# Two-layer graph attention: scores and aggregates by one level of Strassen, VectorE's side work in small pieces

## Chip, cores, metric

One core of one Trainium2 chip. The metric is the device time of one execution, in microseconds (us); each kernel ran several times on one chip with the kernel before.

## The reference, cut to what matters

N = 2708 nodes, D = 1024 features, all float32; adj is an N x N 0/1 matrix.

```python
h = relu(layernorm(x))
e = relu((h @ Wf + bf) @ (h @ Wg + bg).T)          # scores, N x N
att = softmax(where(adj > 0, e, NEG), axis=1)
x = x + att @ (h @ W0 + bW)                         # layer 0
h = relu(layernorm(x))
g = h @ W1
e = leaky_relu(g @ a1 + (g @ a2).T)                 # layer 1: scores are a sum of two vectors
x = x + relu(softmax(where(adj > 0, e, NEG), axis=1) @ g)
```

Both kernels work out `q = h Wf Wg^T` once, scores as `q h^T`, and take the product with W0 or W1 after the aggregate (`(att h) W`). So three large products run over N x N x D: the scores, and one aggregate in each layer.

## The kernel before

Nodes are cut into six panels of columns (four of 512, two of 330) and 22 tiles of up to 128. A panel's scores need 22 x 8 matmuls, and so does each aggregate.

```python
# rows: 6 buffers of 4 KB a partition, slots: 74 of 2 KB
for p in range(NP):                       # preamble, panel by panel
    ...                                   # load x, normalise, transpose: hp
    ...                                   # project: q_ps -> q_ev -> q_d in DRAM
    ...                                   # load adj, convert (nm), transpose: mask in DRAM

def scores(p):
    for t in range(NT):
        nc.sync.dma_start(hT[:, :, :n], hT_d[t][:, :, :n])
        ps = bank("s_ps")
        for k in range(NC):
            nc.tensor.matmul(ps[:n, :w], hT[:, k, :n], q[k][:, :w], ...)
        nc.vector.tensor_tensor(s, ps, nrb, OP.max)      # then + mask, then running max
    ...

def aggregate(l, p, Pt, then={}):
    for c in range(NC):
        ps = bank("g_ps")
        for t in range(NT):               # cut: loads of hc
            nc.tensor.matmul(ps[:, :w], hc[:n, t - t0, :], Pt[t][:n, :w], ...)
        copy(g[:, :w], ps[:, :w])
    ...

def finish0(r):                           # after the projection of each tile of layer 0
    ...                                   # residual, store, normalise for layer 1,
    ...                                   # dots with a1 and a2, running max over the masks

for p in range(NP):
    scores(p + 1); aggregate(0, p, ...); project(p, ..., finish0)
```

## Time and profile before

| | before |
|---|---|
| time, median | 3790.3 us |
| PE busy / DVE busy | 94% / 34% |
| scores of one panel, 512 / 330 columns | 151.1 / 97.9 us, PE never idle |
| first scores begin / second panel's scores begin | 582 / 789 us |
| from an aggregate's last matmul to the projection's first | 4.9 to 5.3 us, ten times (weights); none at two narrow panels |

The profile's lines for this stand in the prediction. PE is TensorE, DVE VectorE, ACT ScalarE, POOL GpSimd, and SP (SyncE) the engine that issues most loads. "s_ps <- q,hT" means: tile s_ps is written from q and hT. A stretch is a slice of time with each engine's busy time in it.

### The profile page before, as it was taken

To read this page: it belongs to the slowest core of one execution; us is meant where nothing else is said; L and a number is where in the kernel's file an instruction comes from. 1 tells how busy PE (TensorE), PEld (TensorE's weight loads), DVE (VectorE), ACT (ScalarE), POOL (GpSimd) and SP (SyncE) were. 2 spreads that over 40 slices of the span, in tenths; PEclk is the share of its full clock that TensorE was granted. 3 is DMA by queue.
4 is the path that set the end of the run, shared out by engine and by line. 5 is a ranking of instruction groups with operands and counts; after the bars stand their busy time and mean duration, and the time that the engine had idled before them with its cause. 6 is when DMAs were issued, how large, how long until landed. Compare 5 with 4: busy or idle time off the path is not lost.

```text
span 3788.7 us, 26140 instructions
## 1 busy us (share of the span) xinstructions
PE 3573.6 (94%) x9800; PEld 1766.4 (47%) x9800; DVE 1276.2 (34%) x2541; ACT 325.6 (9%) x563; POOL 298.5 (8%) x440
## 2 busy tenths in 40 slices
PE   6988889779999999999999999997999999999999
PEld 3444464334444444444464466562444444444655
DVE  4133342453326233522442163309605033030400
ACT  1011210100100010001001001001101010010100
POOL 0133451000000000000100010100000000000000
PEclk8999989889999999999999999998999999999999
DMA  4175574322244224322542453443333322333433
GB/s 155 43 265 190 193 222 134 114 81 89 77 142 139 82 77 153 129 81 76 176 140 74 140 161 103 153 162 115 101 118 104 120 88 93 105 95 119 143 124 106
DMA packets 182783, 472.06 MB, mean 125 GB/s; under 512 B 33652, under 2 KB 57260, under 8 KB 182656
## 3 DMA queue, kind: packets, MB, share of 16 engines
q1 hardware_dynamic: 156096, 388.26, 31.5%
q0 software_dynamic: 26560, 82.13, 6.2%
q8 instruction: 77, 1.26, 0.1%
q14 instruction: 50, 0.41, 0.0%
HBM read 388.20 MB, written 82.10 MB: 124 GB/s over the span
## 4 chain that ended last, share of the span: by engine, by line
PE 90%; DVE 5%; DMA 2%; issue 1%; ACT 0%; SPq 0%; POOLq 0%; POOL 0%; ACTq 0%; DVEq 0%
PE g_ps L324 41%; PE s_ps L389 21%; PE o_ps L342 15%; PE q_ps L233 8%; PE M_ps L175 3%; DMA w<-in_L_gnn_W_dram 1%; DVE junk L153 1%; DVE bn L185 1%; PE mk_ps L258 0%; DVE sm L311 0%; DVE junk L211 0%; DVE P L515 0%; DVE h L191 0%; DMA wf<-in_L_gnn_Wf_dram 0%; DVE P L516 0%
## 5 line engine op out<-in xcount | busy, mean ns | idle before, releaser
L324 PE MATMUL g_ps<-P,hc 128*128 128x512 f32 (+3 forms) x2112 | 815.0, 546 | 8.5 <-ACT P L517 8.5
L324 PE MATMUL g_ps<-S,hc 128*128 128x512 f32 (+3 forms) x2112 | 808.7, 543 | 0.0
L389 PE MATMUL s_ps<-q,hT 128*128 128x512 f32 (+3 forms) x2112 | 803.5, 543 | 0.6 <-DMA q<-q_d 0.6
L342 PE MATMUL o_ps<-w,gT 128*128 128x512 f32 (+1 forms) x1408 | 629.2, 610 | 51.9 <-DMA w<-in_L_gnn_W_dram 51.9
L324 PEld LDWEIGHTS g_ps<-P,hc 128*128 128x128 f32 (+1 forms) x2112 | 398.8, 191 | 399.2 <-issue 318.3
L389 PEld LDWEIGHTS s_ps<-q,hT 128*128 128x128 f32 (+1 forms) x2112 | 393.4, 187 | 406.9 <-issue 337.7
L324 PEld LDWEIGHTS g_ps<-S,hc 128*128 128x128 f32 (+1 forms) x2112 | 398.3, 190 | 383.3 <-issue 323.0
L342 PEld LDWEIGHTS o_ps<-w,gT 128*128 128x128 f32 (+1 forms) x1408 | 266.9, 191 | 412.5 <-issue 377.0
L102 DVE COPY gT<-g_ps 128x512 f32<-128x512 f32 (+1 forms) x48 | 30.0, 625 | 810.8 <-PE g_ps L324 810.8
L233 PE MATMUL q_ps<-hp,M 128*128 128x512 f32 (+1 forms) x768 | 301.0, 556 | 0.7 <-DVE nr L213 0.6
L391 DVE TENSOR_TENSOR S<-s_ps,nrb 128x512 f32<-128x512 f32 (+2 forms) x132 | 82.8, 627 | 484.8 <-PE s_ps L389 484.6
L233 PEld LDWEIGHTS q_ps<-hp,M 128*128 128x128 f32 x768 | 150.3, 197 | 148.2 <-issue 123.2
L102 ACT COPY gT<-g_ps 128x512 f32<-128x512 f32 (+1 forms) x48 | 25.6, 533 | 1769.0 <-PE g_ps L324 1742.7
L533 DVE TENSOR_TENSOR o<-o,x_res 128x1024 f32<-128x1024 f32 (+1 forms) x22 | 27.0, 1225 | 408.2 <-ACT o L532 408.2
L442 POOL DMA_DIRECT2D x_d<-x_res x22 | 12.5, 568 | 1862.8 <-DVE x_res L441 1857.7
L452 DVE SCALAR_TENSOR_TENSOR junk<-hn,wab 128x512 f32<-128x512 f32 (+1 forms) x88 | 114.5, 1336 | 0.7
L227 POOL DMA_DIRECT2D hT_d<-hp x176 | 105.0, 604 | 118.8 <-ACT hp L102 97.3
L175 PE MATMUL M_ps<-wgT,wfT 128*128 128x512 f32 x256 | 113.1, 604 | 0.0
L534 POOL DMA_DIRECT2D out_dram<-o x22 | 11.7, 534 | 1175.2 <-DVE o L533 1175.2
L441 DVE SCALAR_TENSOR_TENSOR x_res<-o_ps,rcol,x_res 128x512 f32<-128x512 f32 (+1 forms) x44 | 32.8, 746 | 209.7 <-PE o_ps L342 209.6
L517 ACT ACTIVATE P<-P 128x512 f32<-128x512 f32 (+2 forms) x132 | 76.2, 580 | 188.7 <-DVE P L516 188.7
L515 DVE SCALAR_TENSOR_TENSOR P<-ub,f,y 128x512 f32<-128x512 f32 (+2 forms) x132 | 89.9, 681 | 0.8
(122 smaller groups left out, 1700.1 us busy)
## 6 DMA issues: line engine op xcount, KB each, us to landing
hc<-h_d SPq DMA_DIRECT2D x192, 704.0 KB
hT<-hT_d SPq DMA_DIRECT2D x120, 512.0 KB
w<-in_L_gnn_W_dram SPq DMA_DIRECT2D x192, 256.0 KB
mask<-mk_d SPq DMA_DIRECT2D x108, 256.0 KB
adj_i<-in_adj_dram SPq DMA_DIRECT2D x40, 512.0 KB
h_d<-h POOLq DMA_DIRECT2D x22, 512.0 KB, 4.4
h_d<-hn POOLq DMA_DIRECT2D x22, 512.0 KB, 5.2
h<-in_x_dram SPq DMA_DIRECT2D x20, 512.0 KB
```

What stands on the lines that cost most here:

```text
L102: (nc.vector.tensor_copy if flip[0] else nc.scalar.copy)(o, i)
L153: nc.vector.scalar_tensor_tensor(junk, ws[e], 1.0, b[:, e * W:(e + 1) * W], op0=OP.mult, op1=OP.mult, accum_out=part[:, e:e + 1])
L175: nc.tensor.matmul(ps, wfT[k][a // 4][:, (a % 4) * P:(a % 4 + 1) * P], wgT[k][b], start=(k == 0), stop=(k == NC - 1))
L227: nc.gpsimd.dma_start(hT_d[first[p] + i][:, c, :n], hp[c][:, o:o + n])
L233: nc.tensor.matmul(ps[:, :w], M[k][b // 4][:, (b % 4) * P:(b % 4 + 1) * P], hp[k][:, :w], start=(k == 0), stop=(k == NC - 1))
L324: nc.tensor.matmul(ps[:, :w], hc[:n, t - t0, :], Pt[t][:n, :w], start=(t == 0), stop=(t == NT - 1))
L342: nc.tensor.matmul(ps[:n], gT[c][:, o:o + n], ws[c][e], start=(c == 0), stop=(c == NC - 1))
L389: nc.tensor.matmul(ps[:n, :w], hT[:, k, :n], q[k][:, :w], start=(k == 0), stop=(k == NC - 1))
L391: nc.vector.tensor_tensor(s[:n, :w], ps[:n, :w], nrb[:n, :w], OP.max)
L452: nc.vector.scalar_tensor_tensor(junk[:n], hn[:n, e * W:(e + 1) * W], 1.0, wab[k][e][:n], op0=OP.mult, op1=OP.mult, accum_out=part[:n, e:e ...
L515: nc.vector.scalar_tensor_tensor(s[:n, :w], ub[:n, :w], f[1][:n, t:t + 1], y[:n, :w], op0=OP.add, op1=OP.max)
L517: nc.scalar.activation(s[:n, :w], s[:n, :w], AF.Exp)
```

## The change

The intent: take seven half-wide products where there were eight, in the three large products, and keep VectorE's added sums from stalling PE by handing its other work out in small pieces. Cut to the core:

```diff
-    slots = ...bufs=74        rows_ = ...bufs=6
+    slots = ...bufs=82        rows_ = ...bufs=5
+    later, credit = [], [0.0]
+    def behind(us):                      # hand out pieces worth about so much of VectorE
+        credit[0] = min(credit[0] + us, 2 * us)
+        while later and credit[0] > 0:
+            cost, go = later.pop(0); credit[0] -= cost; go()
...
+    def pair_h(l, t, hb):                # partner tile two panels away: stored, loaded again
+        ha = row("ha")
+        nc.sync.dma_start(ha, h_d[l][pairs[q][0]])
+        ls = left_sums(...)              # four DVE sums, seven operands
+        for m, s in ls.items():
+            nc.gpsimd.dma_start(hg_d[l][:, m, :, q, :], ...)
...
 def scores(p):
+            def product(m, ps, start):
+                A = slot("As", (P, NH, P))
+                nc.sync.dma_start(A[:, :, :n], hs_d[i][:, m, j, :, :n])
+                for k in range(NH):
+                    nc.tensor.matmul(ps[:n, :h], A[:, k, :n], B[m][k // 2][:, k % 2, :h], ...)
+            product(M1, X, True)         # seven products into three banks,
+            ...                          # eight half-wide evictions on VectorE
+            behind(4.0)
...
 def aggregate(...):                      # likewise seven products; behind(3.0) after each chunk
...
 def finish0(r):
-            normalize(hn, xt, n) ...     # at once
+            later.append((3.5, norm)); later.append((3.0, dots))
+            later.append((2.6, lambda: pair_h(1, t, xt)))
+            if k: later.extend(running_max(q))
...
-    for p in range(NP): normalise, project, masks
+    for a, b in pair_panels:             # two panels at a time
+        transposed_h(a), transposed_h(b); pair_hT(...)
+        project_q(a), project_q(b); transposed_mask(a), transposed_mask(b)
+    # the last pair is projected between the first scores and the second
```

Each pair of tiles now needs seven score operands of 256 KB (As).

## The prediction

> **What bounds the kernel now.** I read the page's head first, then the chain of work that ended last (by line, then in order of time), then the groups kept apart by form, the waits, and a table of stretches.
>
> ```profile
> span 3788.7 us, 26140 instructions
> ...
> PE 3573.6 (94%) x9800; PEld 1766.4 (47%) x9800; DVE 1276.2 (34%) x2541; ACT 325.6 (9%) x563; POOL 298.5 (8%) x440
> ...
> PE 90%; DVE 5%; DMA 2%; issue 1%; ACT 0%; SPq 0%; POOLq 0%; POOL 0%; ACTq 0%; DVEq 0%
> PE g_ps L324 41%; PE s_ps L389 21%; PE o_ps L342 15%; PE q_ps L233 8%; PE M_ps L175 3%; DMA w<-in_L_gnn_W_dram 1%; DVE junk L153 1%; DVE bn L185 1%; PE mk_ps L258 0%; DVE sm L311 0%; DVE junk L211 0%; DVE P L515 0%; DVE h L191 0%; DMA wf<-in_L_gnn_Wf_dram 0%; DVE P L516 0%
> ```
>
> TensorE is on the chain for 90% of the span, and 62% is exactly what the change shrinks: both aggregates (g_ps) and the scores (s_ps). The chain in order of time gives the pitch without pipelining in it (start, us, what, count):
>
> ```profile
> 1157.77 151.07 PE s_ps L389 x352
> ...
> 1347.50 94.45 PE g_ps L324 x220
> ...
> 2327.86 61.13 PE g_ps L324 x220
> ```
>
> A panel's scores are 8x22 = 176 matmuls in the code and 352 in the trace: each fp32 matmul is two passes. A pass takes 151.07/352 = 0.4293 us at 512 columns (four panels), 61.13/220 = 0.2779 at 330 (two panels). The line through both is 0.832 ns a column plus 3.4 ns. The stretches (core 0: us, then busy us and count by engine, PEclk, DMA share, GB/s):
>
> ```profile
> 170.00:225.00 55.00, 55.00 (x132) 24.44 (x130) 8.19 (x13) 5.48 (x9) 19.92 (x37) 1.00 0.65 239
> 225.00:249.00 24.00, 12.99 (x122) 11.44 (x121) 20.98 (x54) 7.78 (x14) 11.36 (x19) 0.67 0.73 231
> 740.00:790.00 50.00, 8.00 (x22) 4.46 (x23) 49.10 (x126) 16.07 (x26) 0.00 (x0) 0.50 0.32 111
> 1158.00:1309.00 151.00, 151.00 (x353) 65.56 (x352) 59.37 (x93) 0.30 (x1) 3.94 (x4) 1.00 0.29 94
> ...
> 2552.00:2665.00 113.00, 85.54 (x193) 34.37 (x191) 97.56 (x189) 17.10 (x28) 9.28 (x10) 0.88 0.32 106
> ```
>
> Row four is a dense stage: PE never idle, VectorE 39% busy. Rows two, three and five are the places where VectorE leads and PE waits: normalising between panels, softmax of the first panel, the turn to layer 1. VectorE is the engine the change loads.
>
> [...] In the column sums, where matmuls are one column wide, successive loads start 110 ns apart:
>
> ```profile
> 2122.46 0.19 PEld L300 LDWEIGHTS sum_ps<-ones,sm 128*128 128x128 f32 x1 [0.24 <-issue]
> 2122.57 0.19 PEld L324 LDWEIGHTS g_ps<-S,hc 128*128 128x128 f32 x1
> ```
>
> So the recorded 0.19 us is latency, not the rate. [...] The trace's PSUM eviction L391 has 691 ns at 512 and 500 at 330[...], so 256 and 165 columns are estimated at 424 and 329. [...]
>
> **The change, part by part.** *Removed:* 7 half-wide products instead of 8 are 7x4x11 = 308 matmuls, 616 passes, a panel. At 256 columns a pass is 0.2164 us: 133.3 instead of 151.1, saves 17.8. At 165 columns 0.1407: 86.7 instead of 97.8, saves 11.1. There are scores and two aggregates: 3x(4x17.8 + 2x11.1) = **280 us**, all on the chain. The eighth (300) is cut by the constant and by nothing else, if loads hide.
>
> *Also removed:* the first layer's projection no longer waits for its weights. The waits put 51.9 us on o_ps <- w in 12 waits, six of them in each layer; the built order now issues these loads some 30 to 50 matmuls ahead in layer 0, but still late in layer 1. **-26**.
>
> *Moved, the preamble.* In the built order VectorE and PE go pair by pair: normalise 8 tiles, project two panels, then masks. Only 5 row buffers are left for x, partner rows and adj, and slots are so full that 22 of a pair's 24 mask conversions stand behind the second projection, where before they ran under it. My times: M starts at 38 (v's dots, which stood before it, go behind) and ends 150; the second panel's tiles then show, 45; first projection at 195 (before: 170). Projections 2x55 = 110, to 305. Masks: 16 subtractions 7 us, then 19 adj loads not yet buffered, 8.8 MB at 265 GB/s (the page's best slice) = 33, so 40, to 345. Eight tiles: per tile 3.1 normalising + 1.6 dots, 16 left sums x0.69, a few copies, 50, to 395. Projections to 505, masks 545, last six tiles 38 and a start, 588: first scores begin when they did before (587), but two panels are still unprojected. Scores 133 plus 10 for left sums whose DMAs hold slots, to 731; two narrow projections 78, to 809; their masks 33; the 32 dots for layer 1, which the built order puts ahead of the next evictions, 23. The second panel's scores begin at 865, before at 790: **+75**, though 18 of the 280 is already in it.
>
> *Added in scores.* Per tile pair VectorE has 8x0.424 + 2x0.745 + 2x0.69 = 6.3 us beside 12.1 us of PE (narrow 4.8 beside 7.9), and up to 4 us of pieces from the previous panel. After a pair's last product some 3.3 us are queued, plus 1.4 of pieces, then 1.4 for the first three evictions, while PE needs the first bank back after three products, 5.2 us (3.4 narrow). It waits about 1 us for the pairs that carry pieces, some 40 in all: **+41**, the weakest term.
>
> *Added in aggregates.* 22 subtractions x0.42 and 20 evictions x0.42, 18 us beside 133: hidden. Reads double to 28 loads of 704 KB a panel, 20 MB: 151 GB/s, narrow 233, with two loads (9.5 or 6.2 us) of lead: hidden.
>
> *Turn to layer 1.* From the last projection (2590) to the end of the first aggregate took 193, of which PE idled about 25. After: 28 + 3 (left sums) to the first weight, 57 for 11 pairs at 5.2 (before 4.5 by the trace, two half subtractions more); PE can do 33 of the 308 matmuls meanwhile, then 275x0.433 = 119: 207. Without these, 193 - 18 = 175. **+32**.
>
> Sum: 865 + (3790.5 - 790) - (280.2 - 17.8) - 26 + 32 + 41 = **3650 us**, 3.7% less.
>
> **Rivals.** *The saving arrives whole.* If the preamble keeps its 790 and VectorE never holds PE: 3790.5 - 262 - 26 = 3500. For it: VectorE is 34% busy, and small pieces are meant for this. Against: row two shows 21 of 24 us of VectorE at exactly the place that doubles. *Weight loads become the bound:* at 0.19 us each the narrow products would take 616x0.19 = 117 instead of 98, three stages and two panels 6x30 = 180 more than assumed: 3830. Against: the 110 ns above. *VectorE becomes the bound of scores:* if each of 66 pairs cost PE 3 us, another 160: 3810, no gain. For it: narrow pairs have 4.8 + 4 beside 7.9. Against: pieces run out after about eight pairs. *DMA:* 233 GB/s in narrow stages plus projection weights may stall loads by 2 to 3 us a panel, +30; the page's 265 GB/s slice says it fits.
>
> **Range and chances.** The 280 is firm (30 at most). The preamble may be 50 better or 50 worse, stalls 0 to 90, the turn +-15. Together about +-80: 3565 to 3730. Two per cent faster is 3715 or less: 0.83; within 2%: 0.14; slower: 0.03.
>
> **What would show it.** Right: g_ps and s_ps passes at 0.216 and 0.141 us pitch in the chain; scores of the second panel starting near 865; PE idle in scores, before a bank is written again, waiting on VectorE, about 1 us, only in the first eight pairs; no wait of o_ps on weights in layer 0. Wrong: a pitch of 0.19 at 165 columns (loads bind); VectorE or DMA as the main link of the chain in scores; mask conversions hidden under projections after all (second scores near 790), which would give 3580; or waits on hc in every product.

## The result, and the profile after

| | before | after |
|---|---|---|
| time, median (4 runs each) | 3790.3 | 3918.2 us |
| ratio | | 1.0337 (95%: 1.0319 to 1.0355) |
| second panel's scores begin | 789 | 945.5 us |
| scores, panels 2 and 3 (512 columns) | 151.2 | 160.8, 160.0 us |
| scores, panels 4 and 5 (330 columns) | 97.9 | 167.0, 182.1 us |
| aggregate in layer 1 from panel 1 on, 512 / 330 columns | 153 / 99 | 135 / 88 us |

A ratio is the mean time of one kernel's runs over that of the other's of the same rounds, so not quite the ratio of the medians. Panels are counted from 0, so the second panel is panel 1. The change is 3.4% slower, not 3.7% faster. The head of the page of the changed kernel:

```profile
span 3913.2 us, 39051 instructions
...
PE 3349.3 (86%) x14552; PEld 2538.0 (65%) x14552; DVE 1685.1 (43%) x3944; ACT 330.3 (8%) x605; POOL 422.4 (11%) x566
```

PE is busy 224 us less and yet the span is longer: the saving was made and then waited away. The products themselves do what was predicted. The chain in order of time (start, us, what, count) in layer 1:

```profile
3067.31 19.01 PE gx L410 x88
...
3639.91 12.33 PE gx L410 x88
```

19.01/88 = 0.2160 us a pass and 12.33/88 = 0.1401; I had 0.2164 and 0.1407. Weight loads don't bind.

The stretches of the changed kernel: the waits before the first and the second scores, then the scores of panels 1, 2, 4 and 5 (us; busy us and count of PE, PEld, DVE, ACT, POOL; PEclk; DMA share; GB/s):

```profile
588.70:623.60 34.90, 0.00 (x0) 0.02 (x1) 10.82 (x25) 0.00 (x0) 25.86 (x41) 0.50 1.03 382
...
897.30:945.50 48.20, 0.87 (x4) 0.48 (x4) 29.19 (x82) 0.71 (x1) 18.52 (x17) 0.50 0.68 240
945.50:1086.30 140.80, 140.78 (x651) 121.29 (x652) 63.68 (x131) 1.17 (x2) 2.48 (x2) 0.99 0.51 155
1279.60:1440.40 160.80, 146.87 (x645) 124.73 (x646) 71.43 (x158) 0.67 (x2) 9.17 (x9) 0.94 0.49 157
1993.60:2160.60 167.00, 112.61 (x645) 105.75 (x646) 76.97 (x200) 0.37 (x1) 21.04 (x23) 0.82 0.63 196
2344.20:2526.30 182.10, 115.35 (x661) 108.90 (x659) 86.76 (x220) 0.78 (x3) 27.56 (x30) 0.79 0.61 190
```

Panel 1, the only one of these without leftover pieces, is dense: 141 us (3.9 of it are the next aggregate's first passes). From panel 2 on, VectorE has more to do and PE waits. In the narrow panels VectorE is busy under half the time, and the DMA engines 63%: no engine is full, and PE still idles for 54 and 67 us. What it waits for in panel 4 (us in total, times, longest):

```profile
PE sx L505 <- DMA As<-hs_d: 36.2, 7, 17.4
PE sz L505 <- DMA As<-hs_d: 23.5, 4, 13.5
PE sz L505 <- DVE st L514: 6.2, 4, 2.3
PE sy L505 <- DMA As<-hs_d: 5.8, 4, 2.6
```

65 of 72 us are score operands that come late, not VectorE; 17.4 of them lie in front of the panel's first pass, the others inside. The load queue in order of time, at the second longest of these waits:

```profile
1993.59 0.32 SPq L503 DMA_DIRECT2D As<-hs_d  x1
2009.57 0.32 SPq L251 DMA_DIRECT2D ha<-h_d  x1
2010.17 0.33 SPq L587 DMA_DIRECT2D x_res<-in_x_dram  x1
2010.56 4.08 SPq L503 DMA_DIRECT2D As<-hs_d  x6
```

SP issues one operand and then nothing for 15.7 us: the next load in its order is the partner row of a piece (ha), which waits for a row buffer that VectorE's left sums still hold. Six operands stand behind it. VectorE in the same time:

```profile
2004.71 0.33 DVE L529 COPY acc<-Sb 128x330 f32<-128x330 f32 x1
2004.95 0.68 DVE L155 SCALAR_TENSOR_TENSOR junk<-x_res,wab 128x512 f32<-128x512 f32 x1
...
2007.47 0.69 DVE L238 TENSOR_TENSOR ls<-ha,x_res 128x512 f32<-128x512 f32 x1
...
2008.86 0.68 DVE L173 TENSOR_TENSOR ls<-ha 128x512 f32<-128x512 f32 x1
```

VectorE's last work for the pair of tiles that PE has just multiplied (L529) ends at 2005.0; only then come, in its order, the piece's dots and left sums. The last of these that reads the old partner row ends at 2009.54, and SP goes on at 2009.57. So at this wait the next pair's operands could not be issued before the pair at work was finished: SP waits for VectorE, VectorE for PE, and then PE for the operands behind SP's waiting load. And the wait costs more than its length (timeline of PE, start, us, count; in brackets the idle time before):

```profile
2003.36 1.28 PE L505 MATMUL sx<-qb,As 128*128 128x165 f32 x8
2018.18 2.57 PE L505 MATMUL sz<-qb,As 128*128 128x165 f32 x8 [13.54 <-DMA As<-hs_d]
...
2022.00 1.28 PE L505 MATMUL sz<-qb,As 128*128 128x165 f32 x8
```

After the wait eight passes take 2.57 us instead of 1.28. The granted clock is 0.50 in the 2.7 us from 2018.2 on and 0.98 in the 7.8 us after them. The same shows after every wait of 4.2 us and more in panels 2 to 5: passes take twice as long (274 against 140 ns at 165 columns), and full speed is back 3.0 to 6.2 us after the wait, leaving out one that another wait soon followed. A wait of 2.3 us, which ended at 2041.8, was followed by passes at half speed too (clock 0.50 from 2041.8 to 2044.6), while after waits of 1.2 to 1.8 us in panel 4 eight passes took 1.39 us.

### The profile page after: what moved, and what is told of

Same layout as the page of the kernel before. It is cut to its first block, busy times and chain, and to the rows that moved or that the text cites. A ratio compares the mean times of both kernels' runs of the same rounds, so it can differ in the third digit from the quotient of the medians. Undisturbed runs are those within 1.5% of the kernel's fastest.

```text
span 3913.2 us, 39051 instructions
## 1 busy us (share of the span) xinstructions
PE 3349.3 (86%) x14552; PEld 2538.0 (65%) x14552; DVE 1685.1 (43%) x3944; ACT 330.3 (8%) x605; POOL 422.4 (11%) x566
## 5 line engine op out<-in xcount | busy, mean ns | idle before, releaser
L505 PE MATMUL sz<-qb,As 128*128 128x256 f32 (+3 forms) x1584 | 363.1, 376 | 93.3 <-DMA As<-hs_d 63.4
L505 PEld LDWEIGHTS sz<-qb,As 128*128 128x128 f32 (+1 forms) x1584 | 294.9, 201 | 134.9 <-DMA As<-hs_d 59.7
L505 PE MATMUL sx<-qb,As 128*128 128x256 f32 (+3 forms) x1056 | 241.2, 375 | 151.9 <-DMA As<-hs_d 137.2
L505 PEld LDWEIGHTS sx<-qb,As 128*128 128x128 f32 (+1 forms) x1056 | 194.2, 199 | 179.8 <-issue 83.1
L410 PE MATMUL gz<-P,hc 128*128 128x256 f32 (+3 forms) x1584 | 310.1, 355 | 0.0
L410 PEld LDWEIGHTS gz<-P,hc 128*128 128x128 f32 (+1 forms) x1584 | 272.3, 190 | 26.5
L505 PE MATMUL sy<-qb,As 128*128 128x256 f32 (+3 forms) x1056 | 230.7, 363 | 18.5 <-DMA As<-hs_d 18.4
L410 PE MATMUL gx<-P,hc 128*128 128x256 f32 (+3 forms) x1056 | 221.6, 372 | 25.6 <-ACT P L693 23.1
L410 PE MATMUL gy<-T,hc 128*128 128x256 f32 (+3 forms) x1056 | 206.8, 356 | 10.3 <-DMA hc<-hg_d 10.3
L410 PE MATMUL gz<-Sa,hc 128*128 128x256 f32 (+3 forms) x1056 | 207.6, 355 | 0.0
L410 PEld LDWEIGHTS gy<-T,hc 128*128 128x128 f32 (+1 forms) x1056 | 183.9, 192 | 29.1 <-issue 10.6
L410 PEld LDWEIGHTS gz<-Sa,hc 128*128 128x128 f32 (+1 forms) x1056 | 181.7, 190 | 17.4
L276 PE MATMUL h_ps<-ident,h 128*128 128x128 f32 (+1 forms) x176 | 37.5, 385 | 89.7 <-DVE h L232 62.4
```

The lines of the kernel that those rows point to most:

```text
L276: nc.tensor.transpose(ps[:, o:o + n], ht[:n, c * P:(c + 1) * P], ident[:n, :n])
L410: nc.tensor.matmul(acc[d][:, :h], hc[:rows_of[q], q, :], right(m, q), start=(start and q == 0), stop=(q == NQ - 1), skip_group_check=True)
L505: nc.tensor.matmul(ps[:n, :h], A[:, k, :n], B[m][k // 2][:, k % 2, :h], start=(start and k == 0), stop=(k == NH - 1), skip_group_check=True)
```

## The experiments

All but e3, e7, e12 and e17 gave the right result. Score times are from a panel's first to its last score pass; with seven loads up to 6 us of that are already the aggregate's passes. Of the total times expected below, those of e5, e6, e11, e12 and e13 came true (e13's without its scores); the others fell between the cases named or outside them.

### e1: no pieces inside the scores

```diff
 def scores(p):
-            behind(4.0)                  # pieces wait until the scores are issued
```

> The changed kernel, but no small pieces are handed out inside the scores; what is left of them is emitted between a panel's scores and its aggregate. Theory A (the pieces' own loads - partner rows, x rows, masks for the running maximum - sit in the one load queue ahead of the score operands and wait there for row buffers): scores of panels 2 to 5 fall from 161, 160, 167, 182 us to about 136 to 141 (wide) and 90 to 95 (narrow); some 20 to 40 us come back in the aggregates; about 3730 us. Theory B (the score operands alone are too many bytes for the DMA engines): narrow scores stay above 120 us, about 3850. Theory C (evictions stand behind pieces on VectorE, as predicted): like A for the scores, but then the side-queue run must change nothing.

3826.5 us, ratio 1.0098. Scores of panels 2 to 5: 147.7, 148.8, 116.0, 126.9 instead of 160.8, 160.0, 167.0, 182.1: 130 us less. The pieces, now all at once ahead of the aggregates, take 40 back there (panels 3 and 4: 8 and 33 us). Stretch of panel 4's scores:

```profile
1969.30:2085.30 116.00, 102.67 (x645) 97.93 (x646) 50.60 (x141) 0.00 (x0) 1.55 (x3) 0.90 0.62 188
```

So the pieces that were to keep PE going cost 92 us. Why they do so, this run doesn't tell.

### e2: the pieces' loads on another queue

```diff
-        nc.sync.dma_start(ha, ...)       # layer 1's partner rows, x rows, masks of the running max
+        nc.gpsimd.dma_start(ha, ...)
```

> The changed kernel with the loads of the side work (partner rows of layer 1, x rows for the residual, masks for the running maximum) issued by GpSimd instead of SyncE; the bytes and VectorE's work are the same. Theory A: PE's waits for score operands in panels 2 to 5 go from some 210 us to under 80, and the second panel's scores start about 17 us earlier; about 3770 us. Theory B (bytes): same bytes, so no change, 3900 to 3920. Theory C (VectorE): no change, 3900 to 3920.

3879.7 us, ratio 1.0242: 39 us faster, not 150. The second scores begin 19 us earlier (in the changed kernel SP stands at an x row from 913.1 to 930.2, with the second scores' q operands behind it), wide scores lose 6 us each, but the narrow ones are 187 and 182. Panel 4's longest waits, of PE and then of VectorE:

```profile
PE sz L505 <- DVE st L514: 36.3, 6, 16.8
```

```profile
DVE mx L573 <- DMA mask<-mk_d: 23.1, 6, 10.0
```

The wait moved: now VectorE stands at a late mask, and the evictions behind it hold PE.

### e3 and e7: one operand load a pair, with and without pieces

```diff
-                A = slot("As", ...); nc.sync.dma_start(A, hs_d[i][:, m, j])
+                if m == M1: A_[0] = slot("As", ...); nc.sync.dma_start(A_[0], ...)
+                A = A_[0]                # wrong on purpose: one operand for all seven products
 # e7: and no behind(4.0) in the scores
```

> Wrong result on purpose: the seven score products of a pair all use the operand of the first, so six of seven operand loads are gone (20 MB to 3 MB a wide panel); all pieces stay. Theory B: the scores of all panels are 133 to 136 us wide and 87 to 90 narrow, and about 3690 us. Theory A: one late load a pair can still hold PE, but a load is now needed every 12 us instead of every 1.7 and reaches further ahead, so perhaps half of the 230 us goes, about 3800. Theory C: the waits stay where they are, but for VectorE: 3900.

> Wrong result on purpose: no pieces inside the scores and one operand load a pair instead of seven. What remains in the scores is the products and their own evictions. If the rest that the run without pieces left in the scores (about 78 us over 133.3 and 86.7) is the operand loads: wide 134 to 137, narrow 88 to 91 us, time about 3770. If it is VectorE's own evictions (6.3 us a pair, 4.8 narrow): wide stays at 141, narrow at 110 to 120, time 3826.

3840.7 and 3789.9 us. Scores of panel 2 / 4 / 5 in us:

| | seven loads a pair | one load a pair |
|---|---|---|
| pieces | 160.8 / 167.0 / 182.1 | 137.9 / 142.7 / 147.9 |
| no pieces | 147.7 / 116.0 / 126.9 | 141.7 / 95.9 / 103.1 |

The figures with seven loads hold some 6 us of the aggregate's passes. Without these, one load a pair takes 17 us from a wide panel with pieces (13.9 to 1.6 us idle), and 18 and 29 us from the narrow ones; without pieces it takes nothing from a wide panel. Without pieces and with one load the narrow scores come to 96 and 103, where the products alone need 87. Both parts are needed for the whole loss, and in the narrow panels pieces are the larger one. Panel 4 with one load and no pieces:

```profile
1970.90:2066.80 95.90, 91.53 (x617) 90.81 (x618) 47.36 (x133) 0.00 (x0) 0.03 (x1) 0.94 0.15 45
```

VectorE's own evictions (47 us beside 96) fit beside the products.

### e6 and e12: without the masks' loads, without the partner rows' loads

```diff
 # e6, running max:
-                mk = load_mask(p, q)
+                mk = zmask               # a constant zero tile; the softmax is only shifted
 # e12, layer 1:
-        ha = row("ha"); nc.sync.dma_start(ha, ...)
+        ha = hb                          # wrong on purpose
```

> The changed kernel, but the running maximum of layer 1 adds a constant zero tile in place of the masks that it loads (the maximum is then over all nodes, which shifts the softmax and should leave the result as it is). All VectorE work and all pieces stay; 66 loads of 165 to 256 KB, each of which needs a free slot, leave the load queue. If these loads are what holds the score operands in the narrow panels: scores of panels 4 and 5 fall from 167 and 182 to about 110 to 120, about 3790 us. If the partner rows and x rows hold it: 155 to 175 stay, about 3900. If VectorE's queue holds it (pieces ahead of evictions): unchanged, 3900 to 3918.

> Wrong result on purpose: the changed kernel, but layer 1's left sums use the tile itself in place of its partner, so the partner rows are not loaded in layer 0's scores; all VectorE work and every other load stay. If the partner rows (which wait for a row buffer and for VectorE, 15 us at a time, at the head of the load queue) hold the scores: panels 4 and 5 fall from 167 and 182 to 110 to 130, about 3810 us. If it is pieces on VectorE or the number of operand loads: 155 to 180 stay, about 3900.

3886.9 and 3915.9 us; narrow scores 162.8 and 174.4, and 162.1 and 178.0. Neither kind of load alone is the cause. In e12 the load that waited 15 us in the timeline above is gone, but the x row behind it in the queue then waited 16.2 us for the same row buffers. I had named the partner rows as the likely culprit; this run refuted it.

### e13: score operands in a queue of their own

```diff
-                nc.sync.dma_start(A[:, :, :n], hs_d...)     # and q_d's parts
+                nc.scalar.dma_start(A[:, :, :n], hs_d...)
```

> The changed kernel with the two operands of the scores (q parts and left sums) loaded from ScalarE's queue, where nothing else loads; all else stays on SyncE. ScalarE is idle in the scores. If the order in SyncE's one queue is the cause (theory A): scores 136 to 140 wide and 92 to 105 narrow, first scores start at 605 to 612 instead of 623.6, second at 915 to 930 instead of 945, about 3730 us. If free slots, bytes or VectorE are the cause: scores stay within 10 us of 161, 160, 167 and 182, about 3890.

3885.6 us, ratio 1.0251. Inside the wide scores PE's idle time falls from 13.9 to 1.0 us (143.0 us long); the narrow ones go to 157 each. But ScalarE's queue has its own waits (ScalarE's normalising stood 10.6 and 8.5 us in front of panel 2's scores and 9.0 in front of panel 4's): the scores now begin 16, 16, 22 and 13 us late (changed kernel: 7, 8, 17 and 0), so the gain is 33 us. For the waits inside the wide panels sharing the one queue is shown as the cause, though 9 of the 13 us come back as a later start; for the narrow ones (54 and 67 us idle inside before, 48 and 45 now) it is a part. The first and second scores begin no earlier (630.0 and 950.7): a queue of their own does not bring these two starts forward.

### e14, e19, e22: side loads and slots

```diff
 # e14: partner rows and x rows on GpSimd's queue, no masks loaded in the running max
 # e19: 87 slots instead of 82, two hc buffers (the aggregates' operands) instead of three
 # e22: e14 with 86 slots and two hc buffers
```

> The changed kernel with partner rows and x rows loaded by GpSimd and no mask loads in the running maximum: now no side load stands in the score operands' queue and VectorE has no late mask to wait for; all pieces' VectorE work stays. If the narrow scores are held by in-order queues standing behind side loads (in the side-queue run VectorE waited 30 us for masks, in the run without masks SyncE waited 25 us for rows): narrow scores fall from 167 and 182 to under 120, wide to about 140, time about 3760. If each of the two runs had already shown all there is (about -6 wide, -5 to -20 narrow): narrow stays over 145, and buffers that the pieces hold, or VectorE's share, are the cause.

> The changed kernel with 87 slots in place of 82 [...], paid for by two aggregate operand buffers instead of three. If free slots hold the score operands: narrow scores fall from 167 and 182 to 120 to 145, wide from 160 to under 150; the aggregates may gain 0 to 5 us each from the lost buffer; about 3830 us. If slots are not it: narrow stays over 160, and the time is 3910 to 3960.

> The run with the side queue and without masks of the running maximum, with 86 slots and two aggregate operand buffers (one slot fewer than the build that did not fit). If what was left there on the load queue was waiting for slots: PE's waits for score operands in a narrow panel go from 32 us to under 12, narrow scores from 162 and 161 to 115 to 140, the rest being evictions behind pieces on VectorE (28 us of waits). If bytes or VectorE alone hold it: narrow stays over 150. The aggregates lose what they lost with two buffers (some 60 us in all), so the total is not the measure here.

3827.1, 3964.3 and 3871.0 us. (e20, e14 with 87 slots, did not fit by 0.75 KB a partition and gave no result.) Narrow scores: e14 171.7 and 169.7, e19 149.5 and 163.1, e22 153.9 and 148.3. More slots take 18 and 19 us from the changed kernel's narrow panels; in e14, where no piece's load was left in SP's queue, they take 18 and 21. The totals of e19 and e22 are 46 and 44 us worse than those of the kernels they start from, though their narrow scores are 37 and 39 shorter in sum: the aggregates miss their third buffer (some 60 us in e19, by e22's expectation); e14 gains its 91 us mostly outside the narrow scores (earlier starts, shorter wide scores). So with every piece's load out of SP's queue the narrow scores stay as long: another wait takes the place of the first (in e14's panel 4, 28 us for VectorE's evictions instead of 6). What is left in e22's panel 4:

```profile
PE sz L505 <- DVE st L514: 30.5, 6, 11.2
PE sx L505 <- DMA As<-hs_d: 12.8, 2, 11.2
```

Operands are down to 16 us, and evictions behind pieces lead. VectorE's timeline at the longest of these waits (start, us; in brackets its idle time before):

```profile
1945.74 0.69 DVE L232 TENSOR_SCALAR x_res<-x_res 128x1024 f32<-128x1024 f32 x1
1948.39 0.81 DVE L231 TENSOR_SCALAR x_res<-x_res,mv,rs 128x1024 f32<-128x1024 f32 x1 [1.95 <-DMA x_d<-x_res]
1949.23 0.69 DVE L232 TENSOR_SCALAR x_res<-x_res 128x1024 f32<-128x1024 f32 x1
1949.84 0.56 DVE L512 TENSOR_TENSOR sm<-sx,rb 128x165 f32<-128x165 f32 x2
```

The first evictions (L512) of a bank that PE finished near 1938 come at 1949.8, behind steps of the running maximum and two tiles' normalising, and one of these stood 1.95 us at a store that still read its row.

### e9 and e17: the preamble, by order and by bytes

```diff
 # e9: the masks of a panel right behind its own projection
-            for p in (a, b): project_q(p, hps.pop(p))
-            for p in (a, b): transposed_mask(p)
+            for p in (a, b): project_q(p, hps.pop(p)); transposed_mask(p)
 # e17, wrong on purpose: only the first of seven operands of each side of the scores is stored,
 # and loaded seven times
```

> The changed kernel with the masks of a panel transposed right behind its own projection, instead of behind both projections of a pair. My prediction charged about 40 us a pair for mask conversions that stand behind the second projection. If that placing is the cost: the first panel's masks take 6 to 15 us and the second's run partly under its projection, second scores start at 880 to 910 instead of 945, and the time falls by 35 to 65 us, to 3855 to 3885. If the DMA engines' bytes (adjacency and left sums) are the cost, the second scores stay at 930 to 945 and the time at 3900 to 3918.

> Wrong result on purpose: of the seven score operands of each side only the first is stored, and it is loaded seven times in place of the others; VectorE, PE and the number of loads stay, but some 30 MB of stores leave the preamble. If the preamble is held by the DMA engines' bytes: masks of the wide pairs take 28 to 34 us instead of 43, first scores start 20 to 35 us earlier and second scores at 870 to 890 instead of 945, time about 3850. If VectorE's or the load queue's order holds it: second scores stay at 930 to 945, time over 3900.

e9: 3950.1 us, 32 slower. The masks still don't run under a projection, since in VectorE's order the sums of q halves (t) stand ahead of the conversions and wait for the projection's end:

```profile
DVE t L173 <- ACT q L303: 61.2, 7, 27.1
```

e17: 3887.6 us. The wide pairs' masks take, from first to last transpose, 36.7 and 37.5 us instead of 43.0 and 42.5; the first scores begin at 600.1 instead of 623.6, the second at 919.3 instead of 945.5. That is less than the 55 to 75 us that I expected if bytes held the preamble. So 26 us of it go with these stores; whether as bytes (382 GB/s in the stretch shown above) or as entries in GpSimd's queue, the run doesn't separate. That queue moved 48 MB by 790 us in the kernel before and 79 MB by 945 us in the changed one.

### e4, e5, e10, e11, e24: Strassen in the aggregates only

```diff
 # e4: scores as before the change (in pair order), preamble panel by panel; pieces as in the change
 # e5: e4 without pieces in the scores
 # e10: e5, with layer 0's end worked out at once, left sums of layer 0 and layer 1's dots
 #      as pieces in the first two scores
 # e11: neighbouring tiles of a panel as partners (no partner loads but one), layer 0's end tile by
 #      tile in the projection, left sums behind the transposes, six rows and 80 slots,
 #      layer 1's dots as pieces in the second scores
 # e24: e11, dots at once between the first and second scores
```

> Strassen in both aggregates only; scores as in the kernel before (full-width products in pair order, operands loaded in two halves), preamble panel by panel as before, pieces handed out as in the changed kernel. Aggregates at 133 and 86.5 us save 2x(4x17.8+2x11.1)=187 us, 26 us of weight waits go, the preamble's second scores start near 800: 3790-187-26+10+20 = about 3610 us if the scores stay at 151 and 98. If the pieces' loads also hold these scores (theory A applies to any operand load on that queue), narrow scores are 110 to 140 and the time 3660 to 3720.

> The aggregates-only kernel (3772 us) without pieces in its scores; what is left is emitted behind a panel's scores; partners still two panels apart and the preamble as there. If the pieces in the scores are most of what separates it from the better hybrid (3584 us): scores of panels 2 to 5 fall from 164, 164, 131, 133 to 153 and 99, some 20 to 40 us come back in the aggregates, 3700 to 3720 us. If the partner rows and the order of the end of layer 0 are most of it: over 3740.

> Strassen in the aggregates only, no pieces in scores 2 to 5 (the end of layer 0 is emitted in the projection, as before the change), the left sums of layer 0 and layer 1's dots handed out in scores 0 and 1, where VectorE and the load queue have room. If pieces in the scores and the crowded preamble were what ate the gain: scores 151 and 98 to 103, aggregates 133 to 136 and 87, second scores start near 780; 3790 minus 187 for the products, minus 60 for weight waits and what they cost in clock, plus 20 for the turn: about 3560 to 3600 us. If finishing inline stalls the aggregates or the scores instead, 3650 to 3720.

> Strassen in the aggregates only, with neighbouring tiles of one panel as partners, so that no partner row is stored and loaded again (one pair excepted); the end of layer 0 is worked out tile by tile inside the projection as before the change; left sums of layer 0 behind the transposes; layer 1's dots handed out in the second panel's scores; six row buffers and 80 slots. If partner rows in the load queue held the earlier hybrid's scores (starts 20, 21, 57 and 66 us late), these four starts fall under 8 us: scores 151 and 98, second scores start at 760 to 800, about 3570 to 3620 us. If the starts stay late, the loads of x rows alone are enough, and 3700 to 3760.

> The better hybrid with layer 1's dots worked out at once between the first two panels' scores, as in the kernel before, instead of in small pieces in the second panel's scores. VectorE has 32 dots of 0.75 us, 24 us, in front of the second scores there: second scores start at 765 to 790 instead of 743, and about 3610 to 3625 us. If the loads of those weights hide under the first scores, 3600.

| | time, us | ratio | scores, panels 2 to 5 | second scores begin |
|---|---|---|---|---|
| e4 | 3771.7 | 0.9953 | 163.5, 163.9, 131.0, 133.4 | 857 |
| e5 | 3710.9 | 0.9792 | 151.3, 151.3, 100.2, 97.9 | 852 |
| e10 | 3820.5 | 1.0078 | 153.1, 153.7, 99.8, 99.4 | 823 |
| e24 | 3632.0 | 0.9584 | 154.1, 153.1, 99.6, 99.6 | 791 |
| e11 | 3584.0 | 0.9456 | 154.3, 154.3, 100.2, 99.6 | 743 |

e4 and e10 missed: they lie 52 and 100 us above the upper end of the slower range that I had expected. In e4 the pieces hold even scores that load four operands a pair; e5 shows it, 61 us. In e10 the scores are dense but begin 20, 21, 57 and 66 us late, with layer 0's end and its loads in SP's order ahead of the next panel's operands: in front of panels 2, 4 and 5 SP stood 25, 30 and 38 us at x rows and partner rows. e11 takes the partner rows away (with order and buffers changed too) and begins 8, 7, 5 and 5 us late. e24 and e11 differ in the dots alone: as pieces in the second scores, where nothing else is handed out, they are worth 48 us. What separates e5 from e24, 79 us, is partners, order and buffers together; no run tells these apart. e11's page and its chain in order of time:

```profile
PE 3379.4 (94%) x12968; PEld 2249.0 (63%) x12968; DVE 1570.2 (44%) x3394; ACT 330.9 (9%) x605; POOL 382.8 (11%) x562
```

```profile
1097.26 154.32 PE s_ps L495 x352
...
2093.02 99.61 PE s_ps L495 x352
```

e11 is 5.4% faster than the kernel before and gives the right result; PE is at 94% again. It gains 206 us: by the pitches the aggregates' products give 187, by e24 the dots 48, and some 29 are lost again elsewhere. (e5's gain is unclear at the 2% line: 0.9776 to 0.9809.) Whether all three products would gain in e11's order, no run tried.

## Why the prediction was wrong

The sum, taken apart as it was built:

| term | predicted | measured | off by |
|---|---|---|---|
| start of the second panel's scores | 865 | 945.5 | +80 |
| scores of panels 1 to 5, waits in front of 2 to 5 included | 573 + 41 = 614 | 815 | +201 |
| all the rest | 2171 | 2152 | -18 |
| whole (predicted: time; measured: span of the profiled run) | 3650 | 3913 | +263 |

(573 = 3 x 133.3 + 2 x 86.7. 815 = the five lengths, 810.7, less 27.6 of aggregate passes among them, plus 32.2 of waits in front of panels 2 to 5.)

*The products: right.* Pitches are within 0.5%, and loads of weights don't bind. The evictions, estimated at 424 and 329 ns (the line through the two that were read, 691 and 500 ns, gives 422 and 327), took 416 to 425 ns at 256 columns and 321 to 331 at 165.

*"Added in scores ... +41, the weakest term": the step that failed.* It counted VectorE's queue alone and said of the loads nothing but that bytes fit. The runs show 242 us instead of 41: 149 idle inside the scores, 32 in front of them, and some 60 that are neither products nor idle; these are mostly passes at half clock (an estimate: PE was busy for 96 us of panels 1 to 5 at half clock by the trace's clock records, half of it lost; PEclk 0.82 and 0.79 in the narrow panels), a term I did not have. Of the 149, waits for VectorE's evictions, all that the term had counted, come to 30 us by the profile's waits (5, 5, 6 and 14 in panels 2 to 5), and late operands to 119. Three premises were false. Loads were taken as hidden if the bytes fit, though each waits its turn in one ordered queue behind the pieces' loads, which wait for buffers: e13 took the wide panels' inside waits away by a queue of their own alone, if partly for later starts. "Only in the first eight pairs" was false: in the narrow panels waits go on nearly to the end (to 2147 of 2161 us in panel 4). And of the pieces only VectorE's time was charged, not their loads and buffers: e1, e3 and e7 show that the pieces and the seven loads together make the loss. How the narrow panels' loss divides between order, slots (18 to 21 us by e19 and e22) and evictions behind pieces (30 us of waits in e22) depends on which wait is taken away first, so I give no split.

*The preamble, predicted 75 later, measured 156 later: mis-sized.* Up to the last transposes (587.7 us, where I had 583) my times were within 15 us: the first projection began at 180 instead of 195, and slower steps used that up (wide masks 45 for 40, from the projections' end). Then first scores began 36 us after the transposes (I had 5, and 10 more inside the scores), two narrow panels' masks took 61 (33), the second scores began 48 us after the masks (23). Of these 80 us, the stores of the left sums and q parts are 26 (e17) and x rows ahead of the second scores' operands 19 (e2). The rest, mostly the narrow masks, where VectorE waits 43 us for adj loads (five row buffers), I tested by no run.

*The turn to layer 1* took 220 us (2790.8 to 3011.3) where I had 207. *Weights:* the prediction read 12 waits, six in each layer, but two of the 12 are of 0.2 us; there are ten of 5 us, five in each layer. Nine of them are gone, not half; the one left is 5.2 us, and a wide projection takes 55.1 us instead of 57.2. These and slightly longer aggregates (135 for 133) are in the -18, which I have not taken apart further. (The prediction also read 587 for the first scores before the change, from a piece of the chain that leaves out their first 12 passes; they began at 582.)

*Rivals.* "VectorE becomes the bound of scores" named the right stage and came near the size (160 more; it was 201) but had the wrong engine: in panel 4 PE waits 6 us for VectorE and 65 for operands. "DMA ... +30" was nearest in kind, but asked for bytes where order and buffers decided. The chance of slower, 0.03, was far too small: each rival was weighed as a full engine, and none as an empty engine that waits.

## What to carry to other kernels

Before counting what a smaller product saves, follow its operands through the ordered load queue: how far ahead each is issued, which buffer it needs, and whose loads stand before it (one waiting load held six operands for 15.7 us here). Put small pieces of side work in a stage with room (the dots in e11, 48 us gained) and not in one that loads an operand every 1.1 to 1.7 us (the pieces in the changed kernel's scores, 92 us lost by e1). And take the part of a change whose operands are few and large first: here the aggregates alone, once partners, order and dots were rearranged for them (e11), gave 5.4%, where all three products lost 3.4%.
